# A planned instruction order, with other assumed durations for TensorE and later puts of the sums

## Chip, cores and metric

The kernel runs on one core of one Trainium2 chip. The metric is the device time of one execution in microseconds, the median of three runs. The inputs are 16 graphs of 1,024 nodes with 64 features each, a dense 0/1 adjacency matrix of 1,024 x 1,024 per graph in float32, a node mask and the weights of four layers.

## The reference

Four layers follow each other, each of the form x = layernorm(x + layer(x)):

```python
# layers 0 and 3: quantile aggregation over a node's thinned-out neighbours
adj_d = dilate(adj, mask)                  # of nodes with over 10 neighbours, some are dropped
agg   = 0.25*q25 + 0.5*q50 + 0.25*q75      # per channel, over the neighbours' values, sorted
y     = (relu((x + agg) @ W1 + b1) @ W2 + b2) * mask
# layer 1
y = adj @ (x @ weight) + bias
# layer 2: attention, with the adjacency added to the softmax
y = gelu(((softmax((x @ W1.T) @ (x @ W2.T).T) + adj) @ x) @ GCN_W)
```

The quantiles are the costly part: each node needs three interpolated order statistics of its neighbours' values, in 64 channels.

## The kernel before, in words

**How the work is staged.** A graph b goes through a stage that makes index lists from its adjacency (`graph_stream`, functions `neighbours`, `both_ways`, `order` and `lists`). Then follows a step of the first quantile layer, the middle layers, and a step of the second quantile layer, which comes two graphs later (`LAG = 2`, line 63). So there are 32 steps n, one for each pair of quantile layer and graph, listed in `layers` at line 1427. In steady state they alternate: an even n is a first layer (l = 0), the following odd n a second layer (l = 1) of a graph two back.

A step does this, with nodes ordered by their number of neighbours:

- POOL fetches, by indirect DMA, the rows of x that the lists name (`fetch_stream`, line 1449): first 50 gathers `hrows` for the 128 nodes with the longest lists, then 85 gathers `rows` in three groups q = 0, 1, 2 for the other nodes (20, 28 and 37 gathers). One gather moves 128 rows of 64 floats. `hrows` is a ring of 8 tiles with two gathers each (`HROWS`, lines 73 and 1459). The `rows` of each group have one buffer (line 1468).
- PE turns each `hrows` tile into a PSUM tile `turned`, and ACT copies it into `cols` (`turn_stream`, line 1495). When the long lists are sorted and weighted, PE adds them up, makes one last product `turned<-ident,tot`, and ACT copies it to `hagg` (line 1559). Only then does the same stream go on to the next step's `hrows`.
- DVE sorts `cols` in two blocks, and after them the `rows` of the three groups, by networks of minimum and maximum (`sort_stream`, line 1589).
- ACT scales the sorted rows and PE adds them up; ACT copies the result to `agg` (`pick_stream`, line 1618).
- POOL puts the sums in place by 8 indirect DMAs into a DRAM tensor `sums` (`put_stream`, line 1433): one from `hagg`, then one, two and four from the `agg` of groups 0, 1 and 2.
- `last_step` (line 1760) waits for all puts of a step, reads `sums` back as `ag`, and does the small dense layers; for l = 0 the layers 1 and 2 follow (`spread_layer`, `attention_layer`).

**What sets the order.** Eight generators ("streams") each yield their instructions in a fixed order. `give_out` (line 260) merges them into one program order, which fixes each engine's queue, since an engine works its queue in order. It keeps an estimated clock for each engine. For the head of every stream it takes the time at which the engine is free and the operands are ready, and gives out the one with the earliest time. The estimated durations come from `Queue.times` (line 214): an instruction's cost on its engine, and how long after that the result is there. A step can also carry a slack, `step.after(ns)`, which makes its readiness count as later in the comparison:

```python
            t = max(free.get(h.engine, 0.0), ready + h.slack)
...
            if best is None or t < best[0] - 1:
                best = (t, i, max(free.get(h.engine, 0.0), ready))
```

The slack enters the comparison alone, not the estimated clock. A put reads `sums` as well, so that each counts from the put before it: one put costs 1,435 ns and its result counts as there 4,000 ns later. Neither the durations nor the slack put a wait into the program; the waits follow from the data and the buffers. All instructions that `give_out` places show in the profile under line 211, so tiles tell them apart.

Of the kernel before, what the change touches and what calls it, by code (L numbers as in the profile page):

```python
# [186 lines left out]
class Queue:  # L187
# [26 lines left out]
    def times(self, name, args, sizes, halves, psum, accum):  # L214
        n, half = max(sizes), all(halves)
        if self.engine == "V":
            rate = 1.9 if name == "tensor_reduce" and n > 256 and not psum else 1.1
            if name in ("tensor_tensor", "tensor_mul", "tensor_add", "tensor_sub") and half and not psum:
                rate = 0.52
            elif name in ("tensor_scalar", "tensor_copy", "memset") and not psum:  # L220
                rate = 0.26 if half else 0.52
            return 75 + rate * n, 120
        if name == "dma_start":
            return 100, 3000 + 128 * sizes[0] * 4 / 100.0
        if self.engine == "A":
            first = 60 if name == "copy" else 180
            return first + 0.82 * sizes[0] + 100 * accum, 150
        if self.engine == "T":
            cols = sizes[0]
            if halves[1]:  # L230
                return max(45, (0.3 if args[0].shape[0] <= 32 else 0.85) * cols), 250
            return max(170, 240 if name == "transpose" else 1.4 * cols), 250
        if self.engine == "G":
            return (1435, 4000) if name == "indirect_dma_start" else (1000, 200)
        raise ValueError(name)
# [603 lines left out]
def listed_path(ctx: ExitStack, tc: tile.TileContext, x, adj, nodemask,  # L839
# [73 lines left out]
    for j in range(NT // FOLD - 1, NT, NT // FOLD):  # L913
        step = FOLD - N + 1 if j < NT - 1 else -N
# [484 lines left out]
    def put(sums, rows, src):  # L1399
        return G.indirect_dma_start(out=sums[:, :], out_offset=bass.IndirectOffsetOnAxis(ap=rows, axis=0),  # L1400
                                    in_=src, in_offset=None)
# [31 lines left out]
    def put_stream():  # L1433
        for n, (l, b) in enumerate(layers):
            k = batches[b]
            yield Wait("hagg", n)
            if n >= SUMS:
                yield Wait("read", n - SUMS)
            k.sums = dram.tile([N, C], F32, name="sums", bufs=SUMS)
            yield put(k.sums, k.node[:, 0:1], k.hagg)  # L1440
            for q, (t0, ntiles, _) in enumerate(TILE_GROUPS):
                yield Wait("sorted", n, q)
                for t in range(ntiles):
                    step = put(k.sums, k.node[:, t0 + t:t0 + t + 1], k.agg[q][:, t])
                    step.reads.append(k.sums.tensor.name)
                    yield step
            events.add(("put", n))

    def fetch_stream():
# [465 lines left out]
    with tc.manual_schedule():  # L1915
        give_out((graph_stream(), turn_stream(), pick_stream(), weight_stream(), middle_stream(), sort_stream(),
                  put_stream(), fetch_stream()), events, 1000, ("lists", EARLY - 1))

        done = features("y")
        nc.vector.memset(done, 0.0)  # L1920
        nc.vector.tensor_tensor(over, over, done[:, 0, 0:1], ALU.max)
        flag = fp.tile([1, 1], I32, name="flag")
        pt = one([1, P])
        nc.tensor.transpose(pt, over, ident)
        nc.vector.tensor_reduce(flag, pt, AX.X, ALU.max)
        nc.vector.tensor_scalar(flag, flag, 0, None, ALU.is_gt)
# [32 lines left out]
```

## Time and profile before

| | |
|---|---|
| median of three runs | 8791.51 us (8773.04 to 8817.0) |
| profiled execution, its own time | 8816.47 us |
| its span, first to last instruction | 8814.6 us |
| granted TensorE clock, mean | 0.644 |
| busy: DVE | 6230.4 us (71%), 16,118 instructions |
| busy: POOL | 4950.8 us (56%), 4,622 |
| busy: PE | 4147.5 us (47%), 20,739 |
| busy: ACT | 2860.0 us (32%), 8,302 |
| mean DMA rate | 57 GB/s |

The profile names a group of instructions by engine, operation and tiles, out<-in. After the first bar stands the busy time in us and the mean duration of one instruction in ns; after the second bar the idle time of the engine just before them, and what ended it. In the list of waits a line tells who waited for whom: us in total, number of times, longest. "issue" is a start for which no wait is seen. "remote" is a wait that a semaphore ended, where the profile finds no instruction that set it at that time.

### The profile page before, as it was taken

The page shows a single profiled execution, that of the slowest core. Times are in us where ns is not written, and L with a number is a line of the kernel's source. Part 1 is how long each engine was busy: PE and PEld are TensorE (multiplying, and loading weights), DVE is VectorE, ACT ScalarE, POOL GpSimd, SP SyncE. Part 2 cuts the span into 40 slices and gives each one's busy share as a digit, 9 for nine tenths or more (in the row PEclk, how much of TensorE's full clock was granted, in tenths as well). Part 3 has the DMA queues.
Part 4 walks back from the last instruction along what each step waited for, and adds up shares of the span by engine and source line. Part 5 has one row for each costly group of instructions (what it writes and reads, how often), then busy time and mean ns, then how long its engine had stood idle before and what let it go on. Part 6 is the DMA issues. An engine that isn't in the chain of part 4 may idle for free. (4 is left out here: it accounts for less than half of the span.)

```text
span 8814.6 us, 76861 instructions
## 1 busy us (share of the span) xinstructions
PE 4147.5 (47%) x20739; PEld 2132.5 (24%) x20739; DVE 6230.4 (71%) x16118; ACT 2860.0 (32%) x8302; POOL 4950.8 (56%) x4622
## 2 busy tenths in 40 slices
PE   4235546535446355454645454364444446262622
PEld 3123223212222222222222222222122222121211
DVE  5557657557577768677886867678586777866686
ACT  2224333333334333333433332333233233221221
POOL 3352463463465546557575755657475574765574
PEclk6556667767657666676766666576666657565655
DMA  2121313113131213122222213123231222121211
GB/s 72 39 69 26 94 41 86 50 37 89 25 82 44 73 41 89 43 48 74 56 75 59 75 42 84 36 58 76 51 77 42 58 62 55 40 59 26 61 32 22
DMA packets 514659, 498.80 MB, mean 57 GB/s; under 512 B 203002, under 2 KB 350538, under 8 KB 513962
## 3 DMA queue, kind: packets, MB, share of 16 engines
q1 hardware_dynamic: 216736, 261.75, 10.0%
q0 software_dynamic: 146944, 150.52, 9.1%
q10 hardware_dynamic: 150538, 81.54, 3.1%
q8 instruction: 168, 2.75, 0.1%
q14 instruction: 273, 2.24, 0.1%
HBM read 393.02 MB, written 102.50 MB: 56 GB/s over the span
## 5 line engine op out<-in xcount | busy, mean ns | idle before, releaser
L211 POOL DMA_INDIRECT rows<-table,idx x2720 | 2948.6, 1084 | 829.1 <-issue 813.3
L211 POOL DMA_INDIRECT hrows<-table,hidx x1600 | 1681.5, 1051 | 830.9 <-issue 431.6
L211 DVE TENSOR_TENSOR spare<-cols 128x192 f32<-128x192 f32 (+15 forms) x1792 | 1013.4, 599 | 177.5 <-ACT cols L211 94.5
L211 DVE TENSOR_TENSOR cols<-spare 128x528 f32<-128x528 f32 (+14 forms) x1632 | 1010.1, 652 | 73.6 <-remote 34.7
L211 POOL DMA_INDIRECT sums<-hagg,node x32 | 33.6, 1050 | 1341.5 <-ACT hagg L211 1340.6
L211 POOL DMA_INDIRECT sums<-agg,node x224 | 272.9, 1218 | 820.8 <-ACT agg L211 646.9
L211 PE MATMUL picked<-rows,ident 128*128 128x512 f32 (+5 forms) x832 | 423.1, 612 | 420.6 <-ACT rows L211 312.4
L211 ACT ACTIVATE rows<-rows,wt 128x64 f32<-128x64 f32 x1856 | 503.9, 350 | 304.0 <-DVE rows L211 207.2
L211 PE MATMUL pi<-below,numbers 128*32 128x200 f16 x4096 | 220.0, 309 | 807.4 <-issue 224.4
L211 DVE TENSOR_TENSOR spare<-rows 128x128 f32<-128x128 f32 (+8 forms) x1056 | 543.3, 539 | 23.8 <-DVE rows L211 4.1
L211 ACT ACTIVATE below<-slot,past 128x1600 f16<-128x1600 f16 x240 | 390.6, 1628 | 436.5 <-remote 181.5
L211 PE MATMUL turned<-cols,ident 128*128 128x440 f32 (+1 forms) x512 | 302.4, 740 | 463.0 <-DVE cols L211 310.7
L211 DVE TENSOR_TENSOR rows<-spare 128x512 f32<-128x512 f32 (+8 forms) x864 | 452.0, 548 | 6.9 <-remote 3.3
L211 DVE TENSOR_REDUCE top<-one 128x1 f32<-128x512 f32 x256 | 174.8, 687 | 300.8 <-remote 176.1
L211 PE MATMUL one<-xt,wt 64*128 64x512 f32 x512 | 322.9, 899 | 112.2 <-DVE top L211 87.0
L211 DVE TENSOR_TENSOR rows<-rows,spare 128x128 f32<-128x128 f32 (+4 forms) x1088 | 348.5, 328 | 37.3 <-remote 7.9
L211 ACT COPY cols<-turned 128x64 f32<-128x64 f32 (+12 forms) x864 | 170.0, 302 | 593.7 <-PE turned L211 338.8
L211 PEld LDWEIGHTS <-numbers 128*32 128x32 f16 x4096 | 104.8, 104 | 1051.8 <-issue 1047.1
L211 ACT ACTIVATE v<-two,before 128x128 f16<-128x128 f32 x1024 | 278.1, 387 | 227.4 <-PE two L211 71.6
L211 PE MATMUL two<-ident,a 128*128 128x128 f32 x992 | 203.9, 373 | 302.9 <-issue 128.8
L211 PE MATMUL turned<-ident,hrows 128*128 128x128 f32 x800 | 237.6, 376 | 203.1 <-DMA hrows<-table,hidx 124.5
L211 DVE TENSOR_TENSOR spare<-spare 128x64 f32<-128x64 f32 (+7 forms) x480 | 316.0, 658 | 19.0 <-DVE rows L211 4.6
(297 smaller groups left out, 9911.6 us busy)
## 6 DMA issues: line engine op xcount, KB each, us to landing
at<-adjt SPq DMA_DIRECT2D x512, 256.0 KB
a<-in_adj_dram SPq DMA_DIRECT2D x128, 512.0 KB
adjt<-at ACTq DMA_DIRECT2D x128, 512.0 KB
rows<-table,idx POOLq DMA_INDIRECT x2720
hw<-hwt SPq DMA_DIRECT2D x64, 440.0 KB
hrows<-table,hidx POOLq DMA_INDIRECT x1600
hwt<-ho ACTq DMA_DIRECT2D x64, 220.0 KB
ag<-sums SPq DMA_DIRECT2D x32, 256.0 KB
```

The source lines that it names most:

```text
L211: return Step(lambda: f(*args, **kw), self.engine, cost, late, reads, writes, "dma" in name)
```

## The change

`Queue.times` charges TensorE products more: float32 1.82 ns instead of 1.4 ns per column (at least 220 ns instead of 170, transposes 312 ns instead of 240), half precision 1.1 instead of 0.85 ns per column (0.39 instead of 0.3 for at most 32 output rows). In `put_stream` the put of `hagg` gets a slack of 40,000 ns, and the first put of each of the three groups 25,000 ns.

```diff
         if self.engine == "T":
             cols = sizes[0]
             if halves[1]:
-                return max(45, (0.3 if args[0].shape[0] <= 32 else 0.85) * cols), 250
-            return max(170, 240 if name == "transpose" else 1.4 * cols), 250
+                return max(45, (0.39 if args[0].shape[0] <= 32 else 1.1) * cols), 250
+            return max(220, 312 if name == "transpose" else 1.82 * cols), 250
...
             k.sums = dram.tile([N, C], F32, name="sums", bufs=SUMS)
-            yield put(k.sums, k.node[:, 0:1], k.hagg)
+            yield put(k.sums, k.node[:, 0:1], k.hagg).after(40000)
             for q, (t0, ntiles, _) in enumerate(TILE_GROUPS):
                 yield Wait("sorted", n, q)
                 for t in range(ntiles):
                     step = put(k.sums, k.node[:, t0 + t:t0 + t + 1], k.agg[q][:, t])
                     step.reads.append(k.sums.tensor.name)
-                    yield step
+                    yield step.after(0 if t else 25000)
             events.add(("put", n))
```

The instructions themselves and what each waits for by its data stay the same; their order on every engine is made anew.

## Prediction

> **What bounds the kernel now.** I read the page's busy times first, then the list of waits, then the timeline of one step, then busy times by window.
>
> ```profile
> PE 4147.5 (47%) x20739; PEld 2132.5 (24%) x20739; DVE 6230.4 (71%) x16118; ACT 2860.0 (32%) x8302; POOL 4950.8 (56%) x4622
> ```
>
> No engine is full. With 32 steps in 8814.6 us a step takes 275 us, of which DVE works 195 and POOL 155. So the order and the waits set the time. The list of waits for POOL:
>
> ```profile
> POOL sums L211 <- ACT hagg L211: 1340.6, 29, 111.6
> POOL sums L211 <- ACT agg L211: 646.9, 67, 35.9
> POOL hrows L211 <- PE turned L211: 217.9, 70, 18.8
> POOL sums L211 <- ACT rows L211: 114.4, 2, 57.7
> ```
>
> The first, second and fourth line are puts that stand in POOL's queue before their data is there: 2101.9 us, with gathers queued behind them. That looks like the gain. The timeline says what the largest one is worth. POOL's rows, then PE's in the same stretch:
>
> ```profile
> 4185.22 0.94 POOL L211 DMA_INDIRECT hrows<-table,hidx  x1 [0.30 <-issue]
> 4233.27 0.98 POOL L211 DMA_INDIRECT sums<-hagg,node  x1 [47.11 <-ACT hagg L211]
> 4234.56 1.07 POOL L211 DMA_INDIRECT hrows<-table,hidx  x1 [0.30 <-issue]
> ```
> ```profile
> 4232.41 0.33 PE L211 MATMUL turned<-ident,tot 64*64 64x64 f32 x4
> ...
> 4239.71 1.06 PE L211 MATMUL turned<-ident,hrows 128*128 128x128 f32 x4
> ```
>
> POOL has issued 10 of the next step's 50 `hrows` gathers and stops for 47 us. PE makes the last product of the old step at 4232.41 and transposes the first new `hrows` at 4239.71, in that order, since both come from `turn_stream`. The ring holds 8 tiles, 16 gathers. So gather 17 can't start before that transpose, wherever the put stands.
>
> The third view is busy time by window. Between the even and the odd steps POOL runs on while the rest stands still:
>
> ```profile
> 4130.00:4190.00 60.00, 1.58 (x24) 0.79 (x24) 12.00 (x44) 3.63 (x5) 42.76 (x45) 0.52 0.17 38
> 6680.00:6735.00 55.00, 0.00 (x0) 0.00 (x0) 0.00 (x0) 0.00 (x0) 41.59 (x45) 0.51 0.15 26
> ```
>
> The columns are PE, weight loads, DVE, ACT, POOL, granted clock, DMA share and GB/s. In the second row nothing works for 55 us but POOL, gather after gather of 0.94 us every 1.25 us. DVE's `slot` instruction waits 59.7 us there for "remote", although PE's last product before it starts at 6677.80; the semaphore that it waits for moves at 6735.24. In the first window things move again as POOL comes to its stop after 4185.22. Five more such windows (4635, 5140, 5665, 6185, 7225) look the same, 370 us in all seven, about 53 us each and one for each graph: some 850 us of the span in 16. I can't name the cause, but the rows say that POOL's next wait ends a standstill.
>
> [...] The row: PE and ACT have 0.00 us of work in the second window. [...]
>
> **The change part by part.**
>
> *Put of `hagg`, slack 40 us.* The two orders, read side by side, show it behind 10 to 16 `hrows` gathers of the next step before, and behind 32 to 42 in most steps after. The 1340.6 us in front of it go. What is late next is gather 17, behind the same product: in the window it could start after about 4240 us, and it did start at 4242.83 (7th after the put), unhindered. So the 1340.6 us come back as waits of `hrows` on PE `turned`, and the net is **0**. It is hidden by nothing else; it is the same wait under another name. Bounds: a gain of the put's own 1.28 us in 29 steps, 37 us; a loss of the 7.3 us between the two PE rows in 29 steps, 212 us. I take 0, which the window's own gather 17 shows.
>
> *Puts of `agg`, slack 25 us.* These waits are 646.9 + 114.4 = 761.3 us, 23.8 per step. After, the first put of a group stands 21 gathers behind the put before it, so that all 8 are through some 75 gathers after `hagg`. What stops POOL then is the first gather into the one buffer of `rows` q, free when PE has read it, shortly before `agg` q is there. In the order this point lies at gathers 51, 71 and 99 of a step; the old puts lay at about 36, 57 to 68 and 76 to 97. The stop moves by about 10 gathers, 1.25 us each: 12.5 us per step that POOL can win where it waited as long, at most 32 x 13 = **416 us**. It helps only where POOL sets the time, which by the windows is the end of a standstill. In the step that leads to the standstill of 4130 POOL idles 6.5 us in front of its `agg` puts (1.38 and 3.64 us are the long ones). 16 standstills end 6.5 us sooner: **-104 us**. Bounds: -416, and 0 if the standstill begins as much earlier as it ends. Each put also issues its DMA later, by 25 to 45 us. The data goes to `last_step`, and I read its rows in the timeline: `ag` is read at 4102, x3 is written at 4410 and the odd step's output at 4452, and the next puts end at 4602. So 150 us per two steps cover the delay; without that cover it would cost up to 45 us per step. SP reads `ag` later and delays nothing behind it that is due within those 150 us.
>
> *Products 1.3 times as long.* No instruction is added. Against the rows (busy us, count and mean of one):
>
> ```profile
> L211 PE MATMUL one<-xt,wt 64*128 64x512 f32 x512 | 322.9, 899 | 112.2 <-DVE top L211 87.0 <-issue 21.2 <-DMA hrows<-table,hidx 2.9
> L211 PE MATMUL picked<-rows,ident 128*128 128x512 f32 x256 | 227.9, 988 | 312.3 <-ACT rows L211 221.0 <-issue 44.7 <-DVE rows L211 19.3
> L211 PE MATMUL pi<-below,numbers 128*32 128x200 f16 x4096 | 220.0, 309 | 807.4 <-issue 224.4 <-ACT below L211 181.6 <-DVE below L211 174.7
> ```
>
> 512 columns were charged 717 ns and are now charged 932; a single one takes 899 or 988, but PE is busy 631 or 890 per product, since they overlap. The 200-column ones go from 60 to 78, and PE is busy 54 for each. So the new figure fits what a consumer waits for, the old one fits the flow on PE. DVE's waits on PE are what it can relieve, as other work is put ahead of the consumer:
>
> ```profile
> DVE top L211 <- PE one L211: 97.1, 81, 4.0
> DVE dg L211 <- PE one L211: 85.0, 6, 26.3
> DVE rs L211 <- PE pi L211: 44.9, 1, 44.9
> DVE rs L211 <- PE one L211: 31.8, 11, 5.6
> DVE each L211 <- PE turned L211: 25.7, 3, 16.3
> DVE hd L211 <- PE one L211: 23.8, 11, 6.2
> ```
>
> Together 308 us. Bounds: all of it, -308; on the other side, products that are given out later make their readers wait, for which the largest row of its kind is ACT `cols` on PE `turned`, 338.8 us, which doubled gives +339. Half of the planned room fits and half doesn't, so I take a quarter of the gain, **-77 us**.
>
> [...] The row: two 512-column products `po` took 1.96 us at 4201.73 and 1.07 us at 4212.48, with a mean granted clock of 0.644 over the run. [...]
>
> The sum: 0 - 104 - 77 = -181 us. From the profiled execution's 8816.5 us that gives 8635; the median is 25 us lower, so that the number to be measured is 8791.5 - 181 = **8610 us**.
>
> **Rivals.**
>
> 1. *More gain: POOL's lead counts in every step.* Then the whole 416 us come off: 8375 us. For it: in seven even steps (10, 12, 14, 16, 20, 22, 26) POOL waits under 8 us for `hagg`, so POOL is nearly the last there. Against it: in the odd ones it waits about 50 us, and a lead only lengthens that.
> 2. *Slower: the transposes of `hrows` come later on PE.* In the new order the 13th transpose of a step stands 115 to 179 products behind the last product of the old step, before 81 to 105 (steps of the second half). That is about 65 products later, at 8814.6 us / 24205 = 0.364 us each 24 us, and through the ring POOL's gathers come as much later. It decides where POOL has no spare time, the seven even steps: 7 x 24 = 168 us, 8960 us; in all steps it would be 740 us. For it: `hrows` already waits 217.9 us on `turned`. Against it: the products in between are mostly short, and DVE has `rows` to sort meanwhile.
> 3. *No change.* Moved puts only rename waits, the standstills end when the ring stops POOL as before, and new order gains and loses alike: 8790 us.
>
> **How the numbers follow.** Chances: my forecast 0.44, more gain 0.08, no change 0.18, slower 0.30. Two signs hold most of it; the forecast's own range is 8450 to 8745, from twice its gain to the edge of no change. The whole range goes from the first rival's 8375 to the second's 8960. A difference under 0.5% is about what a measurement can't tell from none. So faster by over 0.5%: 0.52, within: 0.18, slower by over 0.5%: 0.30.
>
> **What would show it.** In the profile after: POOL `sums` on ACT `hagg` near zero and POOL `hrows` on PE `turned` up by about as much as that lost, to over 1000 us, is the first step; if POOL's waits shrink by over 1000 us in all, it was wrong. `sums` on ACT `agg` should fall to under 200 us. Standstills of 45 to 55 us, one per graph, should still be there; if they are gone or doubled, my sum is wrong by hundreds of us. DVE's waits on PE by name should be under 308 us. If `ag` is what `last_step` waits for in every step, the cover of 150 us wasn't there.

## The result, and the profile after

| | before | after |
|---|---|---|
| median | 8804.26 us (8773.04 to 8827.47, 4 runs) | 9339.81 us (9238.61 to 9464.28, 4 runs) |
| ratio | | 1.0505 [1.0442, 1.0568] |
| profiled execution, its own time (span) | 8816.47 us (8814.6) | 9255.13 us (9253.3) |

The change makes the kernel slower. The forecast of 8610 us and the whole range up to 8960 us missed. Every ratio in this text leaves out disturbed executions, those over 1.5% above the fastest of the same kernel; of the four after these are 9424.49 and 9464.28 us, which is why the median is higher than the ratio says.

The page after, busy time of each engine. DVE does the same work as before (6223 us against 6230), in a longer span:

```profile
PE 4355.1 (47%) x20739; PEld 2171.3 (23%) x20739; DVE 6223.0 (67%) x16118; ACT 2847.3 (31%) x8302; POOL 4899.3 (53%) x4622
```

The list of POOL's waits after (who waited for whom: us in total, times, longest):

```profile
POOL hrows L211 <- PE turned L211: 1976.5, 106, 128.1
...
POOL rows L211 <- PE picked L211: 239.5, 13, 33.3
POOL sums L211 <- ACT hagg L211: 115.5, 3, 87.5
POOL sums L211 <- ACT agg L211: 92.5, 12, 22.2
```

The puts' waits are gone, as meant: 1340.6 to 115.5 us and 646.9 to 92.5 us. In their place stand waits in front of the gathers, and POOL waits more in all. But POOL is not what got slower. Busy time by window shows what did. These are 10 us stretches of the changed kernel; the columns are PE, weight loads, DVE, ACT, POOL (busy us and instructions), granted clock, DMA share, GB/s:

```profile
6554.00:6564.00 10.00, 9.07 (x29) 2.77 (x27) 9.63 (x18) 10.00 (x32) 8.17 (x7) 1.00 0.44 102
6564.00:6574.00 10.00, 7.73 (x35) 4.36 (x34) 9.93 (x27) 8.39 (x39) 7.70 (x8) 0.79 0.12 24
6574.00:6584.00 10.00, 6.22 (x44) 5.48 (x43) 5.93 (x15) 2.90 (x11) 7.72 (x8) 0.67 0.12 25
6584.00:6594.00 10.00, 0.34 (x2) 0.10 (x1) 0.00 (x0) 0.00 (x0) 7.56 (x9) 0.50 0.16 28
6594.00:6604.00 10.00, 0.00 (x0) 0.00 (x0) 0.00 (x0) 0.00 (x0) 7.56 (x9) 0.50 0.13 26
6604.00:6614.00 10.00, 0.00 (x0) 0.00 (x0) 0.00 (x0) 0.00 (x0) 7.56 (x9) 0.50 0.13 26
6614.00:6624.00 10.00, 0.00 (x0) 0.00 (x0) 3.06 (x18) 0.00 (x0) 7.55 (x8) 0.50 0.13 26
```

POOL began a run of gathers and puts without a break at 6554 and ended it at 6624. In its first 20 us DVE is full. From 6584 on, DVE, PE and ACT stand, for over 30 us. This is the standstill that the prediction read in the profile of before and expected to find again, "one per graph". Four rows of the timeline show how it ends:

```profile
6620.94 0.95 DVE L211 TENSOR_SCALAR slot<-two 128x400 f16<-128x400 f32 x3 [40.88 <-remote]
6622.74 0.94 POOL L211 DMA_INDIRECT rows<-table,idx  x1 [0.30 <-issue]
6630.13 0.59 ACT L211 COPY side<-picked 128x512 f32<-128x512 f32 x1 [51.26 <-remote]
6630.77 2.08 PE L211 MATMUL picked<-side,ident 128*128 128x256 f32 x4 [45.48 <-ACT side L211]
```

The POOL row is the last gather of the run. DVE starts again shortly before it, ACT and PE only 6.5 and 7 us after its end. There are more standstills now.

To count them I took from the traces POOL's **unbroken runs**: DMA issues that each begin less than 1 us after the end of the one before (any other instruction of POOL breaks a run). Before has 34 such runs of over 60 us, about two for each graph; after has 50, about three. So 16 more, one per graph, for 9255.1 - 8816.5 = 439 us: 27 us for each. DVE's idle gaps of over 10 us say the same: 57 of them with 1189 us before, 75 with 1709 us after.

### The profile page after: what moved, and what is told of

The parts are those of the page before. It is cut to its first block, busy times and chain, and to the rows that moved or that the text cites. A ratio compares the mean times of both kernels' runs of the same rounds, so it can differ in the third digit from the quotient of the medians.

```text
span 9253.3 us, 76753 instructions
## 1 busy us (share of the span) xinstructions
PE 4355.1 (47%) x20739; PEld 2171.3 (23%) x20739; DVE 6223.0 (67%) x16118; ACT 2847.3 (31%) x8302; POOL 4899.3 (53%) x4622
## 5 line engine op out<-in xcount | busy, mean ns | idle before, releaser
L211 POOL DMA_INDIRECT rows<-table,idx x2720 | 2905.4, 1068 | 1116.0 <-issue 808.6
L211 ACT ACTIVATE rows<-rows,wt 128x64 f32<-128x64 f32 x1856 | 525.6, 356 | 187.0 <-DVE rows L211 96.9
L211 DVE TENSOR_SCALAR below<-slot 128x1600 f16<-128x1600 f16 x272 | 157.0, 582 | 482.8 <-remote 331.1
L211 PE MATMUL one<-xt,wt 64*128 64x512 f32 x512 | 404.2, 1045 | 86.9 <-DVE top L211 76.8
L211 PEld LDWEIGHTS picked<-rows,ident 128*128 128x128 f32 x832 | 187.8, 275 | 988.4 <-ACT rows L211 730.3
L211 PEld LDWEIGHTS <-near 128*128 128x128 f16 x3072 | 183.0, 112 | 703.5 <-issue 647.4
L211 PE MATMUL po<-at,y 128*64 128x512 f32 x512 | 295.2, 778 | 107.7 <-DMA at<-adjt 49.2
L211 POOL DMA_INDIRECT sums<-agg,node x224 | 251.7, 1123 | 170.2 <-ACT agg L211 92.2
L211 PE MATMUL pu<-e,x 128*65 128x512 f32 x512 | 302.2, 680 | 81.7 <-ACT e L211 50.2
```

What stands on the lines that cost most here:

```text
L211: return Step(lambda: f(*args, **kw), self.engine, cost, late, reads, writes, "dma" in name)
```

## The experiments

Three theories. **1, products:** the longer assumed products spread the small products of the middle layers, and that chain grows until it sets the end. (In the trace of after, the even step 14 takes 478 us from the read of the sums to the written x3, against some 310 before. Between the output of an odd step and the end of the next even step's last put, 14 to 58 us of room are left in steps 14 to 26, against 123 to 153 before.) **2, late puts:** the sums reach the middle layers later. **3, stops:** a long unbroken run of POOL brings the others to a stand; the waits in front of the puts were the stops that ended or prevented one, and the slack took them away.

**Each part alone.** The edits are those of the change, one part at a time. All four ran on one chip, where before takes 8554.99 us (8465.67 to 8622.82).

Products alone:

> The products are assumed 1.3 times as long, the puts have no slack. Theory 1 (the assumed durations alone spread the small products of the middle layers and what reads them, so that the chain from the read of the sums to the written x3 grows from about 310 to about 480 us and sets the end): about 9250 us, at least 1.04 times before. Theory 2 (the slack of the puts does it, since the read of the sums comes later): 8700 to 8850 us, within 1% of before. If both share it: about 9000.

Both slacks:

> Both slacks of the puts, with the old assumed durations. Theory 1 (durations): 8700 to 8850 us, and POOL's waits in front of the put of hagg under 150 us with as much back in front of hrows. Theory 2 (slack): at least 9200 us. Theory 3 (POOL's longer runs of gathers without a pause make the standstills longer): slower too, 9000 to 9300, with the summed standstills up from 1115 us to some 1450 us.

The slack on the put of `hagg` alone:

> The slack of 40 us on the put of hagg alone. By the prediction's first step the wait is only renamed: within 0.5% of before. Theory 1: the same. Theory 2: the put is given out about 40 us behind its data, so the read of the sums comes as much later in each step; where the chain of the middle layers has 150 us of room per two steps this costs nothing, where it has not it costs up to 16 x 40 = 640 us. Theory 3: the pause in front of this put is the longest that POOL has, so most of the loss would be here, 9000 us or more.

The slack on the puts of `agg` alone:

> The slack of 25 us on the first put of each group alone. The prediction's second step: 104 us faster, 8690 us. Theory 1: within 1% of before. Theory 2: the last put of a step, and with it the read of the sums, comes some 25 us later: 0 to 16 x 50 us slower. Theory 3: slower by less than the put of hagg alone, since these waits are 761 us and not 1341.

| kernel | time, us | against before | unbroken runs over 60 us |
|---|---|---|---|
| products | 8714.95 | 1.0121 [1.0061, 1.0181] | 36 |
| both slacks | 9358.61 | 1.0916 [1.0826, 1.1007] | 51 |
| slack on `hagg` | 8663.01 (8530.98 to 8719.43) | 1.006, from two runs | 31 |
| slack on `agg` | 9167.62 (8998.00 to 9224.38) | 1.054, from one run | 49 |

The last two ratios rest on so few runs that they have no interval; by the medians of all runs they are 1.013 and 1.072. Theory 1 falls as the main cause: the products alone cost a little over 1%. The put of `hagg`, which had the largest wait, costs no more, so theory 3 as I first put it ("most of the loss would be here") falls too. Its wait came back under the name that the prediction gave:

```profile
POOL hrows L211 <- PE turned L211: 1118.8, 103, 81.2
...
POOL sums L211 <- ACT hagg L211: 193.5, 3, 88.5
```

Here POOL still stops, now in front of gather 17 of a step (802 us in 19 waits of over 5 us), and the long runs number 31. The puts of `agg` make most of the loss, and with them the long runs go from 34 to 49. Late data or missing stops? Both fit so far. Both slacks together cost more on this chip (9.2%) than the whole change did elsewhere (5.1% above, 5.5% below). The whole change was not run on this chip, so it stays open whether the chips differ or the longer products win something back beside the slacks.

**Stop kept, put late.** To tell the two apart, POOL copies one element per partition of `agg` at the place of the old put, without slack, and the put keeps its slack. So POOL stops for `agg` as before the change, and the sums come as late as with it:

```diff
                 yield Wait("sorted", n, q)
+                yield G.tensor_copy(slot_no[:, 0, 0:1], k.agg[q][:, 0, 0:1])
                 for t in range(ntiles):
...
-                    yield step
+                    yield step.after(0 if t else 25000)
```

(`slot_no` is a constant that nobody reads after the start. In this kernel and the ones with writes below, an instruction of POOL other than a gather or put is charged 400 ns instead of 1,000.) Its first run met a surprise: on that chip the kernel before takes 7010.67 us (7005.45 to 7033.96), a fifth less than on the others, and the trace of this kernel shows next to no standstills (DVE's gaps of over 10 us: 15 with 205 us). So it tells nothing about them, but much about the chip:

> The slack of 25 us on the puts of agg, but POOL copies one element per partition of agg, without slack, ahead of each group's first put: so POOL stops for agg where it stopped before the change, and only the puts themselves are late. Theory 3: what counts is the stop, so about as fast as before, within 2%. Theory 2: the puts are as late as in the run with the slack alone, so 5 to 8% slower.

It took 7083.87 us, 1.0094 [1.0062, 1.0125]. The same kernel was then run on another chip, beside the changed kernel and the slack on `agg` alone:

> The changed kernel itself, since the chips differ: the four runs before this one were made on a chip on which the kernel before takes 7010.67 us and the trace shows no standstills at all (90 us of slices with little work against 1115). If this chip has no standstills either: theory 3 says that the change costs little there, 0.99 to 1.02 times before; theory 1 (spread products) at least 1.03, since a longer chain of the middle layers needs no standstill. If this chip has them: about 1.05 again.

> The slack of 25 us on the puts of agg alone, again. On a chip without standstills: theory 3 says 0.99 to 1.01 times before, theory 2 (late puts) at least 1.03. On a chip with them: 1.06 to 1.08 by both.

> The slack on the puts of agg, with POOL stopping for agg by a copy of one element where it stopped before the change. On a chip with standstills: theory 3 says at most 1.02 times before, with standstills about one per graph as before; theory 2 says 1.05 to 1.08. On a chip without them it took 1.0094 times before, and should again.

| kernel (before: 8819.53 us) | time, us | against before | runs over 60 us | DVE idle, us |
|---|---|---|---|---|
| changed kernel | 9325.64 | 1.0554 [1.0478, 1.0630] | 47 | 3059 |
| slack on `agg` | 9329.77 | 1.0552 [1.0478, 1.0626] | 49 | 3150 |
| the same, stop kept | 8933.78 | 1.0106 [1.0051, 1.0161] | 32 | 2714 |

Theory 2 falls. In step 16 the last put of the kernel with the stop kept comes 50 us after the copy to `agg` (5202 to 5252), later than the 21 us (5382 to 5403) with the slack alone, and still four fifths of the loss are gone. The same holds over steps 4 to 29: the last put comes 49 us (median) after the last copy to `agg` with the stop kept, 21 us with the slack alone. The long runs are down to 32, and DVE's gaps of over 10 us from 1708 to 1311 us.

The kernel with the stop kept was recorded on both chips, which shows what a standstill is. Two runs that start with the same gathers of a step, one graph apart, first on the chip with standstills (run from 6044.57 to 6173.68), then on the one without (5054.15 to 5194.47); columns as above:

```profile
6055.00:6075.00 20.00, 17.34 (x36) 6.00 (x36) 19.69 (x49) 6.85 (x11) 16.34 (x13) 0.83 0.26 66
...
6155.00:6174.00 19.00, 1.11 (x4) 0.71 (x4) 5.71 (x22) 3.24 (x9) 14.21 (x15) 0.50 0.56 150
```
```profile
5074.00:5094.00 20.00, 18.26 (x46) 7.11 (x45) 19.73 (x36) 6.91 (x12) 16.38 (x12) 1.00 0.26 66
...
5174.00:5194.00 20.00, 13.11 (x74) 9.68 (x74) 19.27 (x52) 10.82 (x34) 15.73 (x15) 0.83 0.88 264
```

Early in the run DVE is full on both. 100 us later DVE works 5.71 of 19 us on the one chip and 19.27 of 20 on the other. Taken over all 32 long runs of each trace, the share of time, in slices of 0.1 us, in which an engine has an instruction:

| time since the run began | DVE, PE with standstills | DVE, PE without |
|---|---|---|
| 0 to 10 us | 0.93, 0.57 | 0.97, 0.64 |
| 40 to 50 us | 0.58, 0.53 | 0.96, 0.57 |
| 60 to 70 us | 0.46, 0.11 | 0.92, 0.56 |
| 90 to 100 us | 0.38, 0.23 | 0.97, 0.69 |

**Stops put in.** If stops are what counts, more of them should help on a chip with standstills. POOL gets small writes (128 x 154 floats, 0.39 us each) into `slot_no` among the gathers:

```diff
+    fetches = itertools.count(1)
+
+    def pause():
+        if next(fetches) % 4 == 0:
+            for _ in range(3):
+                yield G.iota(slot_no, pattern=[[0, 7], [1, MOST]], base=0, channel_multiplier=0,
+                             allow_small_or_imprecise_dtypes=True)
...
                     yield fetched(table, rows[:, h, :], k.hidx[:, h, g:g + 1])
+                    yield from pause()
...
                     yield fetched(table, rows[:, s, t, :], k.idx[:, c:c + 1])
+                    yield from pause()
```

It was run first on the chip without standstills, then on one with them:

> The kernel before, with POOL given three small writes of 0.39 us each (iota into a tile that nobody reads any more) behind every fourth gather, 34 times a step; the plan charges 400 ns for each. Theory 3 (standstills are what an unbroken run of gathers does to the others' semaphores, and a stop of POOL ends them): if 1.2 us without a gather is enough to let semaphores through, the standstills fall from 1115 us to under 500 and the kernel gets 3 to 6% faster; if it is too short (in the traces things move again only some 6 us after POOL's last gather), nothing but POOL's 34 x 1.2 = 40 us more per step is seen, 0 to 3% slower. Theory 2 (late puts): no gain either way.

> Three small writes of POOL, 1.2 us, behind every fourth gather. On a chip without standstills they cost 1.15 times before, 1065 us for 1266 us of writes, so POOL sets the time there. On a chip with standstills theory 3 says that they pay for themselves, 0.94 to 1.02 times before, with the standstills under 500 us; theory 2 says 1.02 to 1.10.

Then with fewer stops, shorter stops, and in the changed kernel; the last two on a further chip:

> The kernel before, three small writes of POOL, 1.2 us, behind every eighth gather instead of every fourth. On a chip with standstills: if the number of stops counts, half the gain of 8% or less, 0.94 to 0.97 times before; if a stop every 10 us is often enough, the gain stays and POOL gets 20 us a step back, 0.88 to 0.92. On a chip without standstills about 1.06, half the loss of 15%.

> One write, 0.39 us and its gaps, behind every fourth gather. On a chip with standstills: if any step without a DMA issue lets the others' semaphores through, 0.88 to 0.92 times before; if the time counts, a third of the gain, about 0.97. On a chip without standstills about 1.05.

> The changed kernel with three writes behind every fourth gather. Theory 3 (the stops are all that the change lost): within 2% of the kernel before with the same stops, so 0.91 to 0.94 times before on a chip with standstills and about 1.15 on one without. If the spread products or the late puts cost time of their own as well: 3 to 5% over the kernel before with the same stops.

> The kernel before with three writes behind every fourth gather, for the comparison in this call: 0.92 times before on a chip with standstills, 1.15 on one without.

> The changed kernel with three writes behind every eighth gather, 17 stops a step. If the stops are all that the change lost: 0.89 to 0.92 times before, within 2% of the kernel before with the same stops (0.9085). If the changed order needs more stops than the old one, since it has lost its own: 0.94 to 0.99. On a chip without standstills 1.03 to 1.08.

> The kernel before with three writes behind every sixteenth gather, some 8 stops a step, 20 us apart. If a stop ends a standstill whenever it comes: 0.90 to 0.94 times before. If 1.2 us is too short to clear what has piled up in 20 us: 0.96 to 1.0. On a chip without standstills about 1.03.

| kernel | stops | time, us | against before | before, us |
|---|---|---|---|---|
| before | 3 writes each 4th gather | 8076.16 | 1.1515 [1.1491, 1.1539] | 7010.67, no standstills |
| before | 3 each 4th | 8110.81 | 0.9181 [0.9131, 0.9230] | 8819.53 |
| before | 3 each 4th | 8092.12 | 0.9250 [0.9200, 0.9300] | 8742.38 |
| changed | 3 each 4th | 8024.21 | 0.9175 [0.9125, 0.9224] | 8742.38 |
| before | 1 each 4th | 7985.37 | 0.9108 [0.9038, 0.9178] | 8742.38 |
| before | 3 each 8th | 7941.42 | 0.9085 [0.9034, 0.9135] | 8742.38 |
| before | 3 each 16th | 8255.97 | 0.9292 [0.9247, 0.9336] | 8896.07 |
| changed | 3 each 8th | 7735.14 | 0.8689 [0.8640, 0.8738] | 8896.07 |

Theory 3 holds: work added to POOL makes the kernel 7 to 13% faster than before in every run on a chip with standstills, and 15% slower on the one without. Two results are faster than any expectation had them, 0.9181 (0.94 to 1.02 expected) and 0.8689 (0.89 to 0.92). With the stops it takes the same 8076 to 8111 us on both kinds of chip. One write of 0.39 us does at least as much as three (0.9108 against 0.9250), so it is not the time that POOL stands which counts. A stop every 20 us (each 16th gather) is still worth 7% (0.9292). Each stop also makes the gathers a little rarer, and no run separates the two. And the changed kernel with stops is no slower than the kernel before with the same stops: 0.9175 against 0.9250 on one chip. So the change costs nothing of its own that shows beside the stops; what it lost was its stops. (The changed kernel without added stops was not run on the chip without standstills.) The last line is the fastest version on a chip with standstills. In its profile, of an execution of 7824.56 us, POOL is busy 5700 us, 634 of them writes, and DVE is busy 80% of the span:

```profile
PE 4309.8 (55%) x20739; PEld 2155.7 (28%) x20739; DVE 6265.4 (80%) x16118; ACT 2863.3 (37%) x8302; POOL 5700.2 (73%) x6242
...
L211 POOL IOTA slot_no<- 128x154 f32 x1620 | 634.0, 391 | 80.7
```

Whether the changed order is also better than the old one with a stop at each 8th gather (0.8689 against 0.9085) stays open, since the two ran on different chips. Two further kernels, with some 8 us of writes behind each 27th gather, one of them with the slack on `agg`, give wrong sums for a reason that I did not find; their times, 8146.21 and 8123.56 us on the chip without standstills, are no evidence.

## Why the prediction was wrong

*Put of `hagg`: right.* The wait was renamed, 1340.6 us to 193.5, and `hrows` on PE `turned` from 217.9 to 1118.8, most of it in front of gather 17, as forecast. The ratio of 1.006, some 50 us, lies within the bounds of -37 to +212.

*Puts of `agg`: wrong, and this is the step that failed.* It gave -104 us with bounds of -416 and 0. Measured: +5.5% [4.8, 6.3], some 487 us of 8819.53. The step said that an earlier POOL "helps only where POOL sets the time, which by the windows is the end of a standstill", and shortened 16 standstills by 6.5 us each. Yet an earlier paragraph had said that "POOL's next wait ends a standstill". The step did not put this to the waits that the change removes: they were such stops, and without them a third long run per graph (50 of over 60 us against 34) reaches its standstill (75 of DVE's gaps of over 10 us against 57). The upper bound of 0 was for a standstill that "begins as much earlier as it ends"; it took for granted that the number of standstills stays. The price was on the page: about 53 us for each, 16 of them 850 us, which would have been the bound of a loss. The measured 27 us per added run lies inside. The other fear, data that is late for `last_step`, was rightly priced at nothing for the slack: with it alone the odd step 17 ends at 5829 and the last put of step 18 is at 5990, 161 us later, where 150 were expected. In the changed kernel that cover is nearly gone (14 to 58 us in steps 14 to 26). As the room is 48 to 97 us in most steps with the products alone and 118 to 169 with the slack alone, the products take it up, not the slack.

*Products: the sign was wrong, the bounds held.* -77 us was taken, -308 to +339 allowed; +1.21% [0.61, 1.81] was measured, some 104 us. The whole change takes as long as the slack on `agg` alone (1.0554 and 1.0552). The quarter of the gain was a guess: "the old one fits the flow on PE" holds for the product on which PE spends 631 ns, not for `picked`, whose 890 ns are nearer to the new 932 than to the old 717. DVE's waits on PE by name were to fall; over all tiles they rose, from 405.5 us before to 505.2 with the products alone and 523.9 after, while the six rows of the prediction fell, from 308 to 255 and 282. Waits of which the profile doesn't find the end count in neither, and the traces are of different chips, so where the 104 us went stays open.

*Standstills.* "If they are gone or doubled, my sum is wrong by hundreds of us" is near to what happened: long runs are up by half, and the sum was wrong by over 600 us.

*The range.* "Twice its gain" would put the lower edge at 8430, not 8450; it made no difference.

*Rivals.* The second named the right side and 8960 us, by another mechanism, late transposes. No run tests it by itself; it is part of the products' kernel and of the put of `hagg`'s, and neither cost more than about 1.2%.

## What to carry to other kernels

Before a wait is taken away, ask what else happens while that engine waits; here POOL's waits in front of its puts were stops that let the other engines go on (without those for `agg` it took 1.0552 times before, with them kept 1.0106), and the bound of zero took for granted that the number of standstills stays. Where the other engines go on after one engine pauses, put a pause in on purpose: it is a cheap experiment, and here it was also the gain, 7 to 13%, though on the chip without standstills it cost 15%.

## What the runs showed of the hardware

**Semaphores late while POOL issues gathers.** In the kernel with the slack on `agg`, PE's products of 128 x 9 go from 33 in 0.98 us to one to four at a time, 0.7 to 1.4 us apart, some 5 us before DVE stops. The last of them starts at 6300.36, and yet the DVE instruction that reads them starts at 6342.53, after 51.87 us of waiting and 6.5 us after the end of POOL's last gather of the run (6336.02). From the timeline, PE's rows, then POOL's and DVE's:

```profile
6284.17 0.98 PE L211 MATMUL one<-later,near 128*128 128x9 f16 x33
...
6288.27 0.17 PE L211 MATMUL one<-later,near 128*128 128x9 f16 x1 [0.52 <-issue]
6288.98 0.18 PE L211 MATMUL one<-later,near 128*128 128x9 f16 x1 [0.55 <-issue]
6289.69 0.17 PE L211 MATMUL one<-later,near 128*128 128x9 f16 x1 [0.52 <-issue]
...
6300.36 0.17 PE L211 MATMUL one<-later,near 128*128 128x9 f16 x1 [1.24 <-issue]
```
```profile
6335.08 0.94 POOL L211 DMA_INDIRECT rows<-table,idx  x1 [0.30 <-issue]
6342.53 0.23 DVE L211 COPY before<-one 128x72 f32<-128x72 f32 x1 [51.87 <-remote]
```

The traces also hold the times at which semaphores moved. In the kernel with the stop kept, on the chip with standstills, a tenth of the recorded updates of PE's semaphore come over 1.65 us after the last PE instruction that sets it, the latest 52 us after. (In the profile of before, from a chip with standstills too, it is a tenth over 1.87 us, the latest after 57 us.) On the chip without, 99 of 100 come within 0.05 us, the latest after 3.6 us.

**It differs between chips.** The kernel before takes 7010.67 us on one and 8554.99 to 8896.07 on the others. All runs on the one were made in a single session, so it is not shown whether the chip itself makes the difference. On the one, DVE goes on while POOL gathers: taken over all 32 long runs of the kernel with the stop kept, DVE has an instruction at least 0.87 of the time in each 10 us after their start.

**Why is open.** On the chip without standstills the trace holds 110,640 semaphore updates of the kernel with the stop kept, 16 for nearly every gather; on the other it holds 51,521 of the same program, so more than half of the records are missing there, and the names of waits are less sure. No run shows whether the recording has a part in the standstills, since every time comes with a recorded span and clock.
